# A two-layer graph network on one core: slot rows sent within SBUF in three parts of 14 slots, and attention one-hots, exponentials and sort halves on ScalarE and in PSUM

## The chip, the core and the metric

The kernel runs on one NeuronCore of a Trainium2 chip as a single program. The metric is the device time of an execution in microseconds. The times are compared as medians of repeated executions. A hardware profile of one execution gives the views that are quoted here. Engines are named as in the profile: PE is TensorE (PEld its weight loads), DVE is VectorE, ACT is ScalarE, POOL is GpSimd and SP is SyncE. POOL does no arithmetic in the loops below: it issues indirect DMAs (gathers of 128 rows by an index per partition).

## The reference

There are 12,500 nodes with 128 features and 200,000 edges, sorted by destination; all arithmetic is f32.

```python
h = relu(layernorm(x))
# layer 0: attention over the incoming edges, 8 heads of 16
q, k, v = h @ Wq.T, h @ Wk.T, h @ Wv.T
score = einsum('ehc,ehc->eh', q[dst], k[src]) / 4 + edge_attr @ We.T
alpha = softmax of score over the edges of one dst
x = x + segment_sum(v[src] * alpha, dst)
# layer 1: three graph convolutions on h = relu(layernorm(x)), 128 -> 256 -> 128 -> 128
#   conv(h) = D^-1/2 (A + I) D^-1/2 (h @ W) + b, then batch norm (and relu after the first two)
return x + that
```

## The kernel before

**Setup.** The nodes are cut into 106 tiles of 118 destinations (`TN`). Layer norm and the three projections run first and leave `q_d` and the joint table `kv_d` in HBM. Each tile has a window of 2048 edges (`WE`, 16 per partition, `JJ`), read at a position that is loaded into a register (L929).

**Attention** is one loop over the 106 tiles, in groups of four. Per tile:

- SP loads the edge features `ebx`, the tile-relative destinations `dw_b` (broadcast over the partitions) and `qt`. POOL issues 16 gathers of 1 KB rows into `kv` (L148). Three buffers of `kv` exist (pool `ga`).
- DVE writes the transposed one-hot `oht` from `dw_b` (L1013, 128x2048). PE spreads the queries to the edges with it (`qe`, L1019, 16 matmuls). DVE multiplies by the keys (L1020, four times 512 elements) and sums per head (L1023).
- PE adds the edge bias (L1036), and a chain of scans on DVE, small matmuls on PE and a copy on ACT finds each destination's maximum (L1051 to L1075).
- ACT writes the exponentials into `vals` (L1081). DVE multiplies the values by them (L1082, 2048 elements), which is the last reader of `kv`.
- DVE writes the one-hot `oh` (L677, called from `one_hot`), and PE sums over the edges (`acc`, L1089, 16 matmuls).

The order on each engine is fixed when the program is built, and each engine runs its own list strictly in order; instructions of neighbouring tiles are interleaved there.

Beside the last 80 tiles or so, **`place_edges`** sorts every tile's edges by source. It is a generator; `go_on(1)` at four places of a tile runs one step each. Its sort is a bitonic network on 106 partitions x 2048 keys, 66 stages, done twice. One stage is one step: a `min` and a `max` of 1024 elements each, both inputs in SBUF (L701, L702). Between the sorts, edges beyond `SB` = 13 per (tile, group of 128 sources) are marked late. Each tile has 98 x 13 = 1274 slots and up to `OV` = 768 late edges.

**Each convolution** (`conv_slots`, three times) works on blocks of nine tiles (`TB`), twelve blocks, with the table `hs` in SBUF:

- `take` (L1221 to L1228): for each of the 98 groups of 128 sources, DVE writes a one-hot `go` (128 x 117), PE multiplies (`gp`), so that row (tile, slot) holds the source's row. ACT copies four groups at a time into `stage`, and each 14 groups are written to a block `m` in HBM.
- `reduce`, for each tile of the block before: three DMAs read the tile's 1274 rows back from `m` into `mr` (L1245, 128 partitions x 10 rows), POOL gathers 6 x 128 late rows from the table in HBM (five buffers), DVE writes one one-hot `oh` of 16 x 118 (L1249), and PE adds 10 slot matmuls (L1253), 6 late ones (L1255) and the tile's own rows (L1159) into `zp`. After three tiles `finish` scales, applies the weights and takes statistics.
- `take` of a block and `reduce` of the block before are emitted interleaved; SP issues all their DMAs from one in-order list.

A f32 matmul stands as two instructions in the profile; "a pair" below is one matmul of the program.

## Time and profile before

| | us |
|---|---|
| median of 14 runs (lowest, highest) | 7413.61 (7369.84, 7436.9) |
| the profiled execution | 7384.13 |
| its span, first to last instruction | 7382.3 |
| attention, about | 190 to 3150 |
| three convolutions, about | 3200 to 7325 |

| busy over the span | us | share |
|---|---|---|
| PE | 4734.2 | 64% |
| DVE | 3410.5 | 46% |
| POOL | 4025.9 | 55% |
| ACT | 1014.7 | 14% |

The mean granted TensorE clock is 0.751 of full speed. The DMA engines move 1051.07 MB, 142 GB/s over the span; HBM sees 773.19 MB read and 272.26 MB written. The largest transfers are `m<-stage` (252 of 784 KB) and `mr<-m` (318 of 560 KB).

A line of the groups reads: line, engine, operation, output<-inputs, count | busy us, mean ns of one | idle time of the engine before it, with what ended it. A line of the windows gives, for a stretch of the span, its length and then the busy time of PE, PEld, DVE, ACT and POOL with the number of instructions in brackets, the granted PE clock, the DMA engines' share and GB/s. A line of the timeline gives start, duration, engine, line, operation and count.

### The profile page before, as it was taken

The numbers are of one execution on the slowest core, as the hardware profiler recorded it, in microseconds if no ns is written. First come the engines' busy times: TensorE is split into PE (matmuls) and PEld (weight loads), VectorE is DVE, ScalarE is ACT, GpSimd is POOL, SyncE is SP. The second block draws the span as 40 slices with busy tenths as digits, with TensorE's granted clock in tenths as the row PEclk, the third lists the DMA queues.
The fourth block names the chain that finished last, engine by engine and source line by source line (L and its number), as shares of the span: only waits on it lengthen the run. The fifth ranks groups of instructions, "written<-read, shape, count | busy, mean of one in ns | idle before, by whom it ended". The sixth has DMA issues, their size and how long they took to land. (4 is left out here: it accounts for less than half of the span.)

```text
span 7382.3 us, 80384 instructions
## 1 busy us (share of the span) xinstructions
PE 4734.2 (64%) x28564; PEld 4380.5 (59%) x28564; DVE 3410.5 (46%) x5972; ACT 1014.7 (14%) x2374; POOL 4025.9 (55%) x3617
## 2 busy tenths in 40 slices
PE   5665666566666666646666666666666666666666
PEld 2555565555556565646666666566666656666666
DVE  6455688878667755523332324223223233223234
ACT  2111111111011111111111110111111111111110
POOL 1566588888777877634444443344444425444443
PEclk8676766666776776678888888777777777778778
DMA  6444444444444445366666665565666656666666
GB/s 177 114 125 117 113 110 112 101 115 109 115 115 114 111 121 129 92 166 170 166 164 165 163 160 162 161 161 153 158 156 162 162 148 163 159 160 159 158 157 173
DMA packets 607714, 1051.07 MB, mean 142 GB/s; under 512 B 191227, under 2 KB 418491, under 8 KB 607201
## 3 DMA queue, kind: packets, MB, share of 16 engines
q1 hardware_dynamic: 464311, 695.85, 34.3%
q0 software_dynamic: 142608, 348.39, 19.5%
q8 instruction: 232, 3.80, 0.2%
q14 instruction: 175, 1.43, 0.1%
q10 hardware_dynamic: 388, 1.60, 0.1%
HBM read 773.19 MB, written 272.26 MB: 142 GB/s over the span
## 5 line engine op out<-in xcount | busy, mean ns | idle before, releaser
L148 POOL DMA_INDIRECT rows<-t_d,srcO x1908 | 1820.9, 954 | 2363.7 <-PE zp L1159 674.5
L148 POOL DMA_INDIRECT kv<-kv_d,srcA x1696 | 2200.7, 1298 | 777.7 <-issue 492.7
L1224 PE MATMUL gp<-hs,go 128*117 128x128 f32 x7056 | 1066.4, 309 | 756.3 <-issue 574.2
L1224 PEld LDWEIGHTS gp<-hs,go 128*117 128x117 f32 x7056 | 965.1, 209 | 842.3 <-issue 684.3
L1253 PE MATMUL zp<-oh,mr 128*128 128x118 f32 x6360 | 1062.2, 339 | 610.5 <-DMA mr<-m 324.4
L1253 PEld LDWEIGHTS zp<-oh,mr 128*128 128x128 f32 x6360 | 1021.2, 252 | 631.8 <-issue 318.1
L1249 DVE TENSOR_TENSOR oh<-nums,dlS 128x1888 f32<-128x1888 f32 x318 | 674.1, 2121 | 1479.8 <-PE zp L1255 1406.8
L1019 PE MATMUL qe<-qt,oht 128*128 128x128 f32 x3392 | 842.0, 412 | 227.0 <-issue 110.2
L1019 PEld LDWEIGHTS qe<-qt,oht 128*128 128x128 f32 x3392 | 769.4, 310 | 269.0 <-issue 165.0
L1221 DVE TENSOR_SCALAR go<-gi,iota_q 128x468 f32<-128x468 uint8 x1008 | 433.9, 456 | 1000.6 <-remote 459.5
L1226 ACT COPY stage<-gp 117x512 f32<-117x512 f32 x1008 | 522.5, 532 | 2290.6 <-PE gp L1224 775.3
L1089 PE MATMUL acc<-vals,oh 128*118 128x137 f32 x3392 | 556.2, 335 | 207.3 <-DVE vals L1082 167.9
L1089 PEld LDWEIGHTS acc<-vals,oh 128*118 128x118 f32 x3392 | 536.1, 230 | 230.7 <-DVE vals L1082 186.0
L1255 PE MATMUL zp<-oh,rows 128*128 128x118 f32 x3816 | 522.4, 287 | 45.7 <-issue 45.5
L1255 PEld LDWEIGHTS zp<-oh,rows 128*128 128x128 f32 x3816 | 496.2, 205 | 53.5 <-issue 52.8
L1020 DVE TENSOR_TENSOR kv<-qe,kv 128x512 f32<-128x512 f32 x424 | 288.1, 684 | 498.7 <-DMA kv<-kv_d,srcA 284.6
L1082 DVE TENSOR_TENSOR vals<-kv,vals 128x2048 f32<-128x2048 f32 x106 | 242.4, 2287 | 104.9 <-ACT vals L1081 61.8
L677 DVE TENSOR_TENSOR oh<-iota_f,dlA 128x1888 f32<-128x1888 f32 x106 | 224.0, 2114 | 126.2 <-remote 77.4
L1058 PE MATMUL ends<-ident,mg 128*8 128x128 f32 x212 | 52.0, 336 | 313.8 <-DVE mg L1053 244.8
L1023 DVE TENSOR_REDUCE sc<-kv 128x128 f32<-128x2048 f32 x106 | 240.8, 2272 | 0.0
L1036 PE MATMUL sm<-wbd,et 128*128 128x32 f32 x848 | 167.6, 351 | 94.1 <-DVE mg L1075 63.2
L1036 PEld LDWEIGHTS sm<-wbd,et 128*128 128x128 f32 x848 | 162.9, 283 | 101.0 <-issue 35.3
(242 smaller groups left out, 3544.1 us busy)
## 6 DMA issues: line engine op xcount, KB each, us to landing
m<-stage SPq DMA_DIRECT2D x252, 784.0 KB
mr<-m SPq DMA_DIRECT2D x318, 560.0 KB
dw_b<-dlb_d SPq DMA_DIRECT2D x106, 512.0 KB
gi<-gi_d SPq DMA_DIRECT2D x252, 204.8 KB
rows<-t_d,srcO POOLq DMA_INDIRECT x1908
kv<-kv_d,srcA POOLq DMA_INDIRECT x1696
ebx<-in_edge_attr_dram SPq DMA_DIRECT2D x106, 256.0 KB
mr<-m SPq DMA_DIRECT2D x318, 75.0 KB
```

The source lines that it names most:

```text
L148: nc.gpsimd.indirect_dma_start(out=o, out_offset=None, in_=table[:, :], in_offset=bass.IndirectOffsetOnAxis(ap=idx, axis=0))
L1019: nc.tensor.matmul(qe[:, k, :], ohv[:, :, j + k], qt, start=True, stop=True)
L1020: nc.vector.tensor_tensor(qk[:, j:j + 4, :], qe, qk[:, j:j + 4, :], op=ALU.mult)
L1036: nc.tensor.matmul(bias[:, 4 * k:4 * k + 4, :].rearrange("p j h -> p (j h)"), et[:, k, :], wbd, start=True, stop=True)
L1082: nc.vector.tensor_tensor(vh[:, :, :, :C], kv[:, :, D:].rearrange("p j (h c) -> p j h c", h=H), vh[:, :, :, C:].to_broadcast([P, JJ, H, C] ...
L1089: nc.tensor.matmul(acc, oh[:, j, :], va[:, j, :], start=(j == 0), stop=(j == JJ - 1))
L1221: nc.vector.tensor_scalar(go[:, :n], gv[:, a:a + n], iota_q, None, op0=ALU.is_equal)
L1224: nc.tensor.matmul(gp[:, i, :], go[:, i].rearrange("p t k -> p (t k)"), hs[:, g * SG + a + i, :], start=True, stop=True)
L1226: nc.scalar.copy(stage[:, a:a + n, :], gp[:, :n, :])
L1249: nc.vector.tensor_tensor(oh, nums.unsqueeze(1).to_broadcast(sh), dlS[:, t, :].unsqueeze(2).to_broadcast(sh), op=ALU.is_equal)
L1253: nc.tensor.matmul(zp[:, i, :], mr[:q, j, :], oh[:q, j, :], start=False, stop=False)
L1255: nc.tensor.matmul(zp[:, i, :], rows[:, j, :], oh[:, RC + j, :], start=False, stop=(j == JO - 1))
```

## The change

There are two halves.

**Attention.** `oht` and `oh` are made by ACT: absolute difference, then relu of one minus it (16 instructions of 118 elements for `oh`, whose bias differs per column). The exponentials go to PSUM (`ex`, in the tile of the bias), are multiplied from there, and are copied to `vals` by ACT afterwards. A sort stage copies the upper operand in two halves to PSUM (`hc`, ACT, 512 elements), and `min` and `max` run on 512 elements with that operand; each half is a step, and `go_on(2)` replaces `go_on(1)`. `acc` has one PSUM buffer instead of two, the bias tile two instead of one.

**Convolutions.** `SB` is 14, `OV` is 704 (the sixth gather has 64 rows); a tile has 98 x 14 = 1372 slots, a block still nine tiles. The 98 groups are cut into three parts of 45, 45 and 8 groups, in pieces of 5, 5 and 1 groups. The rows of a piece go by one SBUF-to-SBUF DMA from `stage` (126 partitions, slot and tile) to `mr` (14 partitions, every ninth or eighth one; the tile lies in the free dimension). There is no block in HBM any more. A part's rows of all nine tiles are one buffer of `mr`, of which there are two. `take` of a part is interleaved with `add` of the part before; `zp` of the block's three groups of tiles stays open in PSUM over the three parts. Gathers, own rows and `finish` come with the third part. The gathers' pool `ga` has three buffers instead of five.

```diff
-SB = 13
-OV = 768
+SB = 14
+OV = 704
+PARTS = ((0, 5, 9), (45, 5, 9), (90, 1, 8))
...
             def swap(lo, hi, lo2, hi2):
-                nc.vector.tensor_tensor(lo2, lo, hi, op=ALU.min)
-                nc.vector.tensor_tensor(hi2, lo, hi, op=ALU.max)
+                n, d = lo.shape[1:]
+                for k in range(2):
+                    cut = ...
+                    hc = ps.tile([P, WE // 4], FP, name="hc")[:NTT].rearrange(
+                        "t (n d) -> t n d", n=max(1, n // 2))
+                    nc.scalar.copy(hc, hi[cut])
+                    yield
+                    nc.vector.tensor_tensor(lo2[cut], lo[cut], hc, op=ALU.min)
+                    nc.vector.tensor_tensor(hi2[cut], lo[cut], hc, op=ALU.max)
...
+            def where_zero(x):
+                nc.scalar.activation(x, x, AF.Relu, bias=ones[:, 0:1], scale=-1.0)
...
-                    nc.vector.tensor_scalar(oht, dw_b, iota_q, None, op0=ALU.is_equal)
+                    nc.scalar.activation(oht, dw_b, AF.Abs, bias=niota[:, 0:1])
+                    where_zero(oht)
...
-                    go_on(1)
+                    go_on(2)
...
-                    nc.scalar.activation(vh[:, :, :, C], mx.rearrange("p h j -> p j h"), AF.Exp)
+                    nc.scalar.activation(ex, mx.rearrange("p h j -> p j h"), AF.Exp)
                     nc.vector.tensor_tensor(vh[:, :, :, :C], kv[:, :, D:].rearrange("p j (h c) -> p j h c", h=H),
-                                            vh[:, :, :, C:].to_broadcast([P, JJ, H, C]), op=ALU.mult)
+                                            ex.unsqueeze(3).to_broadcast([P, JJ, H, C]), op=ALU.mult)
+                    nc.scalar.copy(vh[:, :, :, C], ex)
...
-                    one_hot(oh, dlA[:, t, :])
-                    acc = ps2.tile([TN, H * (C + 1) + 1], FP, name="acc")
+                    for j in range(JJ):
+                        nc.scalar.activation(oh[:, j, :], iota_f[:, :TN], AF.Abs, bias=dlA[:, t, j:j + 1], scale=-1.0)
+                    where_zero(oh)
+                    acc = ps1.tile([TN, H * (C + 1) + 1], FP, name="acc")
...
+                def take(b, part, mr):
+                    _, n, pieces = PARTS[part]
+                    rows = mr[:pieces * SB, :, :n, :].rearrange("(k q) t c d -> q k t c d", k=SB)
+                    for _, q, m in batches[part]:
...
+                        stage = sg.tile([TS, MB, D], FP, name="stage")
+                        for a, c in groups(w, 4):
+                            go = gx.tile([P, 4, SB, TB], FP, name="go")
+                            nc.vector.tensor_scalar(go[:, :c], gv[:, a:a + c], iota_q, None, op0=ALU.is_equal)
+                            gp = pg.tile([TS, 4, D], FP, name="gp")
+                            for i in range(c):
+                                nc.tensor.matmul(gp[:, i, :], go[:, i].rearrange("p k t -> p (k t)"),
+                                                 hs[:, s0 + a + i, :], start=True, stop=True)
+                            nc.scalar.copy(stage[:, a:a + c, :], gp[:, :c, :])
+                        for i in range(m):
+                            nc.sync.dma_start(rows[q + i], stage[:, i * n:(i + 1) * n, :])
+                        yield
...
+                def add(b, part, mr):
...
+                        if part == 0:
+                            zps[t0] = pz.tile([P, GN, TN], FP, name="zp")
...
+                        if last:
+                            tg = own_rows(wk, table, t0, n)
+                        for t in range(t0, t0 + n):
...
+                            if last:
+                                rows = ga.tile([P, JO, D], FP, name="rows")
+                                for j, (_, r) in enumerate(over):
+                                    gather(rows[:r, j, :], table, srcO[:r, t, j:j + 1])
+                                nc.tensor.matmul(zp, tg[:, t - t0, :], ident[:TN, :TN], start=False, stop=False)
+                            for j in range(w):
+                                nc.tensor.matmul(zp, mr[:K, t % TB, j, :], oh[:K, j, :], start=False, stop=False)
+                            for j, (_, r) in enumerate(over if last else []):
+                                nc.tensor.matmul(zp, rows[:r, j, :], oh[:r, w + j, :], start=False,
+                                                 stop=(j == JO - 1 and t == t0 + n - 1))
+                            yield
+                        if last:
+                            finish(wk, t0, n, zps.pop(t0), use, ph)
...
+                for b in range(NBK):
+                    for part in range(len(PARTS)):
+                        mr = mt.tile([P, TB, MC, D], FP, name="mr")
+                        done = 0
+                        for g, _ in enumerate(take(b, part, mr)):
+                            while done < g * TB // (len(batches[part]) - 1):
+                                next(tiles, None)
+                                done += 1
+                        for _ in tiles:
+                            pass
+                        tiles = add(b, part, mr)
```

`place_edges` writes the slot indices in the new order (28 stores instead of 12), and the destinations of the slots in the order of the parts.

## The prediction

> **What bounds the kernel now.** I read the page first (shares, slices, groups), then windows of the two stages, the timeline inside each, the waits, and last the order of instructions of both kernels. The chain that ended last says nothing here: it is the output's last 0.5 us. No engine is busy over 64% of the span, so each stage is read by itself. The groups that carry it:
>
> ```profile
> L148 POOL DMA_INDIRECT rows<-t_d,srcO x1908 | 1820.9, 954 | 2363.7 <-PE zp L1159 674.5 <-PE gp L1224 519.7 <-issue 514.0
> L148 POOL DMA_INDIRECT kv<-kv_d,srcA x1696 | 2200.7, 1298 | 777.7 <-issue 492.7 <-DVE vals L1082 195.8 <-DVE rs L1122 51.2
> ```
>
> The reader is to see that one gather takes 954 ns in the convolutions and 1298 in the attention, though it issues the same 128 rows. The windows (attention before, during and after the sort; then one convolution):
>
> ```profile
> 200.00:800.00 600.00, 375.95 (x1858) 341.69 (x1858) 313.96 (x722) 73.63 (x262) 362.19 (x329) 0.70 0.46 117
> ...
> 1000.00:1800.00 800.00, 493.87 (x2488) 449.43 (x2488) 656.43 (x1003) 90.90 (x252) 666.25 (x440) 0.66 0.42 109
> ...
> 2600.00:3000.00 400.00, 268.21 (x1371) 241.60 (x1370) 226.41 (x426) 50.70 (x135) 294.86 (x247) 0.70 0.46 122
> ...
> 4900.00:5700.00 800.00, 519.22 (x3528) 500.08 (x3526) 233.87 (x303) 115.18 (x220) 364.73 (x383) 0.76 0.60 159
> ```
>
> POOL is the fifth of the pairs. Between two gathers stand 0.30 us in which POOL waits for nothing (the timeline's "[0.30 <-issue]"), so a gather occupies its duration plus 0.30. During the sort that is 666 + 440 x 0.30 = 798 of 800 us: **POOL is full**, at 28 tiles (L1082 runs 28 times there), 28.6 us a tile. After the sort it is 295 + 74 = 369 of 400, 26.7 us a tile. Before it, 362 + 99 = 461 of 600: there POOL waits for `kv` buffers, so the chain of PE, DVE and ACT sets the pace. Why gathers are slow shows in the timeline:
>
> ```profile
> 749.76 0.94 POOL L148 DMA_INDIRECT kv<-kv_d,srcA  x1 [0.30 <-issue]
> ...
> 750.51 1.28 DVE L1013 TENSOR_SCALAR oht<-dw_b,iota_q 128x2048 f32<-128x2048 bf16 x1
> ...
> 751.00 2.35 POOL L148 DMA_INDIRECT kv<-kv_d,srcA  x1 [0.30 <-issue]
> ...
> 753.66 0.95 POOL L148 DMA_INDIRECT kv<-kv_d,srcA  x1 [0.30 <-issue]
> ```
>
> The gather that falls on DVE's L1013 takes 2.35 us instead of 0.95. The same stands beside L677, L1082 and the sort's L701 and L702, which also read SBUF twice or at double rate; beside L1249, one of whose inputs lies in PSUM, gathers stay at 0.94.
>
> In the convolutions nothing is full (PE 65%, POOL 365 + 115 = 480 of 800, DMA 0.60). A block of 98 groups has 196 instructions of L1224, and 1384 of them lie in these 800 us: 7.06 blocks, **113 us a block**, 36 blocks. It is a loop of waits: the block goes to HBM and back, PE waits for `mr<-m` (up to 8.7 us at once in the waits), cools, and runs at half rate after it:
>
> ```profile
> 5206.08 4.59 PE L1253 MATMUL zp<-oh,mr 128*128 128x118 f32 x20 [6.16 <-issue]
> ...
> 5212.44 2.40 PE L1253 MATMUL zp<-oh,mr 128*128 128x118 f32 x20
> ```
>
> The same ten pairs cost 0.46 us each cold and 0.24 warm.
>
> **Attention: the parts.** *Removed from DVE, per tile:* L1013 1.28 and L677 2.11 us. L1082 stays at 2048 elements (2.29). A sort stage was 1.21 + 1.21 us, four a tile, 9.7; it becomes four instructions of 512, for which L1020 (512 elements, one input in PSUM, 684 ns) is the nearest row: 4 x 4 x 0.68 = 10.9. During the sort DVE has 656/28 = 23.4 us a tile now, so 23.4 - 3.4 - 9.7 + 10.9 = 21.2 then.
>
> *Added to ACT, per tile:* the rows are L1365 (354 elements with a bias per partition, 591 ns) and L1226 (512 elements 585, 256 elements 374, so 0.82 ns an element). That makes 591 + 1694 x 0.82 = 1.98 us for 2048 elements, twice; 0.40 for 118, sixteen times; 1.85 for 1888; 0.43 for the copy (L1081): 12.6 us. ACT has 90.9/28 = 3.2 now, so 15.8, and during the sort 8 copies of 0.585 more: 20.5.
>
> *POOL:* 16 x (0.945 + 0.30) = 19.9 us a tile if nothing slows it; PE has 494/28 = 17.6 at the clock granted now. Over all 1696 gathers the slowing costs 2201 - 1696 x 0.945 = 598 us: the most that attention can gain while POOL sets the pace.
>
> During the sort four engines then stand at 18 to 21 us and hand work to each other in order; `hc` has one buffer, so copy and min/max alternate. The tile can't be under 21.2; at 28.6 nothing is gained. I take 25, the middle: 34 tiles x 3.6 = **-122 us**. The sort still takes 33 tiles (twice the steps, twice the rate). After it, 48 tiles: slowed gathers cost 295 - 247 x 0.945 = 62 us on 15 tiles, 4.1 each; the waits for `kv` (31 us of 400) stay, and `place_edges`'s remaining steps, which keep both operands in SBUF, still slow some. I take 2.5: **-120**. Before the sort, 24 tiles: the chain sets the pace, DVE loses 3.4 us, ACT gains 12.6 and stands in it (`oht`, `th`, the exponentials, `att`, all in order): I take 0, between -3.4 and +4 (one ACT instruction of 2 us ahead of each of two links of the chain). Sum **-240**. Bounds: -598, and +240 if every copy of the sort waits 1 us behind a one-hot (21.2 + 8 = 29.2, no gain on 34 tiles) and the other 72 tiles get 3 us longer.
>
> **Convolutions: the parts.** *Removed:* per block 14 stores to HBM and 27 reads. *Added:* 26 SBUF-to-SBUF transfers, 126 x 98 x 512 B = 6.3 MB instead of 2 x 5.9. The row nearest to their rate is the hardware queue's total, 695.85 MB for 34.3% of 16 engines' span, 17.2 GB/s an engine; 6.3 MB is then 23 us of a block: hidden. *PE:* 98 + 9 x 18 = 260 pairs a block instead of 251. *DVE:* three one-hots a tile, 17 x 118 elements instead of 16 x 118, 30% busy: hidden. SP issues 49 DMAs a block instead of 57, but its list is in order, and in it the second part's pieces stand behind own-row loads that wait for PE.
>
> [...]
>
> *What is late next:* all 54 late gathers of a block now serve its third part, with three buffers. Three tiles are fetched ahead; the other six come one by one: 5 x 1.245 + 1.10 (64 rows; between 0.77 for half and 1.245) = 7.3 us, so 44, and about 5 for the last one's landing and its 8 pairs: **49 us** from the first tile's rows to the ninth's. By the order of instructions 108 pairs lie inside this stretch, 152 outside it. A pair costs 519/1764 = 0.294 us at the clock mix of now, so 32 (hidden) and 45. The second part's rows can only be sent when the third part of the block before has been read (three parts, two buffers), and PE then waits for the last copy and transfer: 6 us, between 0 and the 8.7 of today's wait, plus a little for two `stage` buffers. 49 + 45 + 6 = **100 us a block** instead of 113. I count 33 blocks, since each convolution's first and last run differently: 33 x 13.3 = **-440**. Bounds: all pairs warm and no wait, 49 + 37 + 2 = 88, -825; all 152 cold and 9 us of wait, 49 + 70 + 9 = 128, +485.
>
> **Sum.** 7384 - 240 - 440 = 6704, said as **6700 us**, against the profiled execution, which is 30 us under the median of the runs shown; that is inside the range.
>
> **Rivals.** *A: only the convolutions gain* (20%). ACT takes DVE's place in the chain. For it: in 200 to 800 POOL isn't the bound at all. Against: during the sort POOL is full and relieved for certain. 7384 - 440 + 0 = 6950. *B: both stages reach their floor* (17%). Cooling ends because PE's gaps shrink, and attention runs at 22 us a tile: 7384 - 500 - 750 = 6130. For it: today's block shows PE warm whenever it has a queue. *C: slower* (11%). One mechanism: the overflow stretch and the other two parts run one after the other, with POOL idle in the second and PE in gaps in the first, so PE stays cold. At 70 us for the 152 pairs plus waits the block is 128; from 120 us a block on, it eats attention's gain. 33 x 15 - 240 = +255 or, with no gain in attention, 7870. *D: gathers aren't relieved* (with A): the scans L1051 and L1078 also read SBUF twice. Against: gathers beside L1051 in the timeline stay at 0.95.
>
> **Chances.** Forecast 50%, A 20%, B 17%, C 11%, no change 2%. A measurement of this kernel can tell about 0.2% from none. Faster 0.87, same 0.02, slower 0.11. The range 6050 to 7400 leaves out C and the bottom of B.
>
> **What would show it.** Mean of the `kv` gathers at 0.95 to 1.05 us instead of 1298 ns: right on the slowing; at 1.2: wrong. L1082's successor running 32 times in 800 us of the sort: 25 us a tile. ACT busy over 55% in attention. 196 instructions of `gp` every 100 us; POOL's waits for `zp` gone from two parts and its gathers back to back in the third; HBM traffic down by some 420 MB. Wrong would be: `rows` waiting on `mr` transfers (SP's order), or DVE waiting for ACT's `hc` most of the sort.

## The result and the profile after

The changed kernel takes 8651.82 us (median of 10 runs, 8622.58 to 8669.75), the kernel before 7407.18 us (47 runs, 7364.33 to 7441.61): a ratio of 1.1674, 95% interval [1.1652, 1.1697]. The forecast was 6700 us and the range 6050 to 7400, so it failed in sign and in range. The profiled execution took 8649.76 us, its span 8648.0, the mean clock was 0.705. Attention ends at 3756 us instead of 3143 (+613), and the rest of the span has 4892 us instead of 4239 (+653): both halves lose.

From the page of the changed kernel, the two groups of gathers and the traffic:

```profile
HBM read 559.41 MB, written 60.93 MB: 72 GB/s over the span
...
L153 POOL DMA_INDIRECT rows<-t_d,srcO x1908 | 1811.5, 949 | 3048.4 <-PE zp L1312 2305.6
L153 POOL DMA_INDIRECT kv<-kv_d,srcA x1696 | 1686.4, 994 | 1889.0 <-DVE vals L1117 1081.7
```

The `kv` gathers fell from 1298 to 994 ns and HBM moves 425 MB less, as foretold; what the change was priced by did happen. But POOL, which was full in the sort, now waits 1889 us ahead of these gathers (778 before), and 3048 ahead of the others. The windows of the changed kernel (before, during and after the sort; then the convolutions; columns as above):

```profile
250.00:800.00 550.00, 278.11 (x1395) 249.53 (x1395) 188.74 (x515) 210.16 (x495) 242.86 (x256) 0.66 0.38 95
1200.00:2000.00 800.00, 410.42 (x2060) 369.66 (x2060) 455.34 (x922) 399.33 (x834) 360.53 (x370) 0.64 0.35 91
2800.00:3600.00 800.00, 437.80 (x2254) 395.09 (x2254) 278.31 (x649) 331.36 (x719) 379.58 (x400) 0.68 0.36 99
5700.00:6500.00 800.00, 515.72 (x3145) 472.28 (x3145) 255.34 (x391) 98.74 (x210) 313.96 (x331) 0.72 0.33 93
```

During the sort no engine is busy over 57%, ACT has 50%. A tile takes 34 us there (28.6 before), a block of a convolution 131.5 (113 before). Something waits for nothing that the page names. The timeline shows it; inside one unbroken run of 32 gathers (3014.7 to 3054.5):

```profile
3033.52 0.95 POOL L153 DMA_INDIRECT kv<-kv_d,srcA  x1 [0.30 <-issue]
3033.93 0.39 PE L1127 MATMUL acc<-vals,oh 128*118 128x137 f32 x1 [1.04 <-issue]
...
3036.07 0.39 PE L1127 MATMUL acc<-vals,oh 128*118 128x137 f32 x1 [1.75 <-issue]
...
3038.89 0.39 PE L1127 MATMUL acc<-vals,oh 128*118 128x137 f32 x1 [2.42 <-issue]
...
3040.30 0.69 DVE L1055 TENSOR_TENSOR kv<-qe,kv 128x512 f32<-128x512 f32 x1 [19.85 <-remote]
...
3058.50 0.29 DVE L1073 TENSOR_TENSOR sc<-sc,sm 128x128 f32<-128x128 f32 x1 [15.19 <-PE acc L1127]
...
3059.91 1.71 PE L1127 MATMUL acc<-vals,oh 128*118 128x137 f32 x6 [0.34 <-issue]
```

The 16 matmuls of `acc` (32 instructions) have nothing to wait for ("issue"). They should follow each other in 0.3 us, as the last six instructions do at 3059.91, once the run of gathers is over. The first 14 still do, from 3029.30 to 3032.9; the next ones in the list come every 2.1 to 2.8 us, and DVE stands still for 20 us for results of PE.

### The profile page after: what moved, and what is told of

The parts are those of the page before. It is cut to its first block, busy times and chain, and to the rows that moved or that the text cites. A ratio compares the mean times of both kernels' runs of the same rounds, so it can differ in the third digit from the quotient of the medians.

```text
span 8648.0 us, 85786 instructions
## 1 busy us (share of the span) xinstructions
PE 5140.9 (59%) x29309; PEld 4613.5 (53%) x29309; DVE 3428.6 (40%) x6812; ACT 2251.6 (26%) x4902; POOL 3502.2 (40%) x3617
## 4 chain that ended last, share of the span: by engine, by line
PE 23%; another core or an unknown queue 15%; issue 9%; DMA 3%; DVE 2%; ACT 2%; POOL 0%; SPq 0%; ACTq 0%; DVEq 0%; POOLq 0%
PE zp L1310 9%; PE gp L1273 6%; PE zp L1312 5%; ACT stage L1275 2%; DMA mr<-stage 1%; PE zp L1308 1%; DVE oh L1302 1%; DMA gi<-gi_d 1%; PE hq L1391 1%; PE tp L1372 1%; DVE go L1270 1%; POOL rows L153 0%; SPq L1277 0%; PE zp L1293 0%
## 5 line engine op out<-in xcount | busy, mean ns | idle before, releaser
L153 POOL DMA_INDIRECT kv<-kv_d,srcA x1696 | 1686.4, 994 | 1889.0 <-DVE vals L1117 1081.7
L1273 PE MATMUL gp<-hs,go 128*126 128x128 f32 x7056 | 1180.8, 326 | 916.7 <-ACT stage L1275 433.5
L1273 PEld LDWEIGHTS gp<-hs,go 128*126 128x126 f32 x7056 | 1048.0, 230 | 1128.2 <-ACT stage L1275 547.4
L1310 PE MATMUL zp<-oh,mr 126*128 126x118 f32 x6996 | 1152.1, 323 | 527.4 <-DVE oh L1302 263.7
L1310 PEld LDWEIGHTS zp<-oh,mr 126*128 126x128 f32 x6996 | 1067.3, 235 | 594.9 <-DVE oh L1302 305.9
L1275 ACT COPY stage<-gp 126x512 f32<-126x512 f32 (+2 forms) x1152 | 536.6, 487 | 3232.2 <-PE gp L1273 1289.7
L1302 DVE TENSOR_TENSOR oh<-nums,dlS 128x590 f32<-128x590 f32 (+1 forms) x954 | 813.2, 853 | 1317.0 <-remote 512.3
L1270 DVE TENSOR_SCALAR go<-gi,iota_q 128x504 f32<-128x504 uint8 (+2 forms) x1152 | 632.3, 569 | 1159.1 <-remote 592.6
L1312 PE MATMUL zp<-oh,rows 128*128 128x118 f32 x3816 | 674.7, 327 | 10.5 <-DMA rows<-t_d,srcO 8.5
L1123 ACT ACTIVATE oh<-iota_f,dlA 128x118 f32<-128x118 f32 x1696 | 513.0, 381 | 6.4 <-issue 6.4
L1117 DVE TENSOR_TENSOR vals<-kv,sm 128x2048 f32<-128x2048 f32 x106 | 241.6, 2279 | 14.7 <-ACT sm L1116 6.5
```

Source lines behind the costliest of these rows:

```text
L153: nc.gpsimd.indirect_dma_start(out=o, out_offset=None, in_=table[:, :], in_offset=bass.IndirectOffsetOnAxis(ap=idx, axis=0))
L1123: nc.scalar.activation(oh[:, j, :], iota_f[:, :TN], AF.Abs, bias=dlA[:, t, j:j + 1], scale=-1.0)
L1270: nc.vector.tensor_scalar(go[:, :c], gv[:, a:a + c], iota_q, None, op0=ALU.is_equal)
L1273: nc.tensor.matmul(gp[:, i, :], go[:, i].rearrange("p k t -> p (k t)"), hs[:, s0 + a + i, :], start=True, stop=True)
L1275: nc.scalar.copy(stage[:, a:a + c, :], gp[:, :c, :])
L1302: nc.vector.tensor_tensor(oh[:, :sh[1]], nums.unsqueeze(1).to_broadcast(sh), dl.unsqueeze(2).to_broadcast(sh), op=ALU.is_equal)
```

## What was asked

I measured this in every trace: **late** is the time from the end of the last recorded matmul that signals a semaphore to a semaphore update of PE that follows more than 0.12 us after it, added up without counting a moment twice. (Ends of matmuls are modelled and some records are missing, so it is rough. Counted from the last matmul of any kind, the 1108 and 2368 us below are 904 and 2049.) The kernels were measured on six occasions; on each of the five after the record, all ran on one chip, and the record doesn't name its chip. They fall into **two conditions**, and without this the numbers can't be read:

| | with hold-ups | without |
|---|---|---|
| occasions | the record; runs 9 to 12; runs 13 to 16 | runs 1 to 4; 5 to 8; 17 and 18 |
| the kernel before | 7407; 7291; 7308 | 6164; 6153; 6149 |
| late, kernel before | 1108 us | 8 or less |
| late, changed kernel | 2368 us | 8 or less |

One chip was in both (runs 1 to 4 and 13 to 16). The spans differ by 7382.3 - 6147.1 = 1235 us for the kernel before and 8648.0 - 6216.8 = 2431 for the changed one, so late is about as long as most of it (1108 and 2368). By stage it is rougher:

| us | attention with / without | cost, late | rest with / without | cost, late |
|---|---|---|---|---|
| before | 3143 / 2950 | 193, 385 | 4239 / 3197 | 1042, 718 |
| changed | 3756 / 2587 | 1169, 1093 | 4892 / 3630 | 1262, 1275 |

Part of a cost can be the clock, which is lower with hold-ups: 0.76 in the prediction's window of a convolution, 0.89 in run 6's. Slower work is not the difference: in the kernel before, a `kv` gather takes 1298 ns with and 1329 without, and L1082 on DVE 2287 and 2286.

The theories:

- **Hold-up.** While POOL issues gathers without a pause, PE's completions come late. Gathers stretched by DVE broke the runs up and so protected the kernel before; the change took that away in attention, and in the convolutions put a block's gathers into one part.
- **The chain through ACT** (my bounds, Rival A): ACT's one-hots and copies simply make a tile longer.
- **The serial stretch** (Rival C): the ninth tile's gathers come after the others, and POOL then idles through two parts.

## The experiments

The runs stand in the order in which they were made. "With" and "without" name the condition.

### 1. A probe of runs of gathers (probe_runs, without)

The probe is a program by itself; it computes nothing of the reference. Its round is four matmuls into PSUM and a DVE copy of 512 elements, 24 times, beside 24 gathers on POOL; stages alter the gathers, here with rests between them.

```diff
+for j in range(24):
+    gather(kv[:, j, :], wide)   # then, by stage: nothing, or an iota
+for _ in range(24):
+    for i in range(4): nc.tensor.matmul(q[:, i, :], ident, rhs, start=True, stop=True)
+    nc.vector.tensor_copy(cp, q)
```

> A measurement by itself: it leaves the whole graph network out. TensorE and VectorE hand one PSUM buffer to each other (four matmul pairs, one copy of 512 elements, 24 rounds a stage) while POOL gathers 128 rows 24 times, in several manners. Theory 1 (a long unbroken run of gathers holds up TensorE's completions): alone a round is about 2 us; beside 24 gathers of 1 KB rows back to back the first five to eight rounds are as when alone, and from about 10 us after the first gather until about 3 us after the last one rounds take 4 us and more; a rest of about 0.4 us behind each gather lessens this, rests of about 1 us, or of 2 us behind each fourth gather, or DVE instructions that slow the gathers, take it away. Theory 2 (the lateness comes from the kernel's own order, the gathers only happen to run then): rounds are within 20% of the lone ones in every stage.

1393.85 us. A round took 2.9 us in every stage, alone or beside gathers: nothing came late. The rests had been moved ahead of the gathers by the order of the program, so they rested nothing. By itself this spoke against the hold-up; it was the first sign of the second condition.

### 2. The attention half alone (attn_half, without)

The kernel before with all hunks of the diff outside `conv_slots` and its constants.

```diff
-nc.vector.tensor_scalar(oht, dw_b, iota_q, None, op0=ALU.is_equal)
+nc.scalar.activation(oht, dw_b, AF.Abs, bias=niota[:, 0:1])
+where_zero(oht)
...
-go_on(1)
+go_on(2)
```

> The attention half of the change alone, convolutions as before. The trace of the whole change has its attention 598 us longer than before (end of the last gather of kv at 3720 instead of 3122 us). If the halves don't act on each other, both theories give 7384 + 600 = 7980 us, with 34 us a tile and kv gathers at 0.95 us. By theory 1 the time in which TensorE's completions are late in attention rises from about 310 to about 950 us; theory 2 says nothing on this.

5801.94 us, 0.9409 [0.9388, 0.9429] of before on the same chip: 362 us faster. The 7980 us that I expected from the record's losses did not come.

### 3. The convolution half alone (conv_half, without)

The changed kernel with the old attention.

```diff
-nc.scalar.activation(oht, dw_b, AF.Abs, bias=niota[:, 0:1])
+nc.vector.tensor_scalar(oht, dw_b, iota_q, None, op0=ALU.is_equal)
```

> The convolution half of the change alone, attention as before. In the trace of the whole change a block takes 131.5 us instead of 113, and the three convolutions 656 us more: 7384 + 656 = 8040 us if the halves don't act on each other. By theory 1 the late time of TensorE's completions is about 130 us in each 500 us of the convolutions instead of 75.

6614.35 us, 1.0726 [1.0705, 1.0748]: 451 us slower, with 8 us late in all. So this half loses by a cause of its own.

### 4. Rests behind each gather (after_rests, without)

```diff
 gather(kv[:, j, :], kv_d, srcA[:, t, j:j + 1])
+rest(pause)          # an iota on POOL
```

> The changed kernel, with work for POOL that nothing needs behind each gather: one iota of 384 elements (about 0.44 us) in attention, four of 16 elements (about 0.13 us each) in the convolutions. POOL so has 16 x 0.45 = 7 us more to do in each tile of attention and 54 x 0.5 = 27 us more in each block. Theory 1: broken runs hold TensorE up less; attention goes from 34 towards 30 us a tile (-400 us), a block from 131.5 to about 122 (-300), 7950 us in all. Theory 2: nothing is won in attention, and the stretch of gathers, which is a block's longest, grows by up to 27 us: 8650 to 9600 us.

8249.76 us, 1.3373 [1.3351, 1.3396]. The test was spoiled: the iotas were gathered into long bunches (from 3500 to 3700 us POOL does nothing else), the first two blocks took 417 and 238 us, the later ones 95.6 as without rests. The 0.44 and 0.13 us expected for an iota follow POOL's iotas in the trace before (0.13 us for 1 element, 0.23 for 128, 1.83 for 2048); here the 9328 iotas took 0.21 us on average. Nothing follows from it.

### 5. The changed kernel again (after_again, without)

No edit.

> The changed kernel once more, beside the kernel before on the same chip. The halves were timed on a chip where the kernel before took 6164 us instead of 7407 and where TensorE's completions were never late. If the lateness belongs to the chip, the changed kernel gives there 6164 - 362 (attention half) + 450 (convolution half) = 6250 us, 1.01 times the kernel before, with conv blocks of about 95 us and attention 360 us shorter; on a chip with the lateness it gives about 1.17 again, as in the first measurement.

6224.26 us, 1.0118 [1.0097, 1.0139]. The halves add up: 6153 - 362 + 451 = 6242. So the same kernel is 1.2% slower in one condition and 16.7% in the other.

### 6. The kernel before, profiled here (before_here, without)

No edit.

> The kernel before, to have its trace from the same chip. Where TensorE's completions are late inside long runs of gathers: 7400 us, blocks of 113 us. Where they are not: about 6160 us, blocks of 82 to 85 us as in the attention half alone, attention as in the convolution half alone.

6148.88 us. Six blocks of a convolution, first of this kernel, then of after_again:

```profile
4215.00:4705.00 490.00, 388.07 (x3012) 379.29 (x3011) 195.09 (x258) 95.76 (x186) 310.13 (x325) 0.89 0.85 219
```

```profile
4097.00:4664.00 567.00, 469.30 (x3143) 426.18 (x3142) 255.53 (x391) 99.03 (x210) 309.61 (x324) 0.83 0.46 131
```

The block before is 490/6 = 82 us, not 113; the changed one is 567/6 = 95. Where they go, in the waits of after_again in this stretch and in its timeline:

```profile
POOL rows L153 <- PE zp L1312: 162.9, 15, 27.8
```

```profile
4104.61 0.96 POOL L153 DMA_INDIRECT rows<-t_d,srcO  x1 [27.41 <-PE zp L1312]
```

A block has a third part of some 52 us (4102 to 4154, from the late matmuls of its first tile to those of its ninth), as long as POOL needs to fetch tiles four to nine, and then some 43 us of the two other parts. In these POOL fetches the next three tiles (its 54 gathers are one run of 68 us, 4104.6 to 4172.5) and then waits 27.4 us at once, for the buffers that only the next third part reads: the serial stretch, with the clock at 0.83 instead of 0.89.

### 7. The late edges spread over the parts (spread, without)

Each part takes the gathers and late pairs of every third tile, so POOL has work in all three.

```diff
+now = t % len(PARTS) == part
...
-if last:
+if now:
     rows = ga.tile([P, JO, D], FP, name="rows")
     for j, (_, r) in enumerate(over):
         gather(rows[:r, j, :], table, srcO[:r, t, j:j + 1])
...
-for j, (_, r) in enumerate(over if last else []):
+for j, (_, r) in enumerate(over if now else []):
```

(The late one-hots have a tile of their own; `ohs` has 3 buffers, `gy` 3 instead of 4.)

> The changed kernel with the late edges' gathers and matmuls spread over the three parts (tile t with part t mod 3) instead of all in the third; the one-hots of slots and of late edges are made apart. Theory 3 (a block of the changed kernel is the stretch in which POOL gathers for all nine tiles, about 47 us, and then the rest, about 48 us, one after the other): with a third of the gathers in each part they lie beside the other parts' matmuls and a block falls from 95 to between 78 and 86 us, 400 us less in all. Theory 4 (the loss is SP's order and the transfers from stage to mr): a block stays at 92 to 98 us.

5706.57 us, 0.9281 [0.926, 0.9302]; late 8 us. The serial stretch is shown: without it a block takes 79 us (six in 472), and POOL's waits for `zp` fall from 162.9 to 63.2 us:

```profile
3936.00:4408.00 472.00, 412.20 (x3138) 385.56 (x3137) 261.08 (x444) 100.36 (x210) 314.03 (x324) 0.93 0.57 157
```

```profile
POOL rows L153 <- PE zp L1313: 63.2, 12, 7.1
```

In this condition it beats both kernels.

### 8. The probe with gathers released by a copy (probe_again, without)

The probe, with stages in which a gather's index is first copied into one of 1, 2, 4 or 8 buffers, which limits the gathers in flight.

```diff
+ix = pool.tile([P, 1], I32, name="ix")
+nc.scalar.copy(ix, idx)
+nc.gpsimd.indirect_dma_start(out=kv[:, j, :], in_=wide, in_offset=...(ap=ix, axis=0))
```

> A measurement by itself; it leaves the whole graph network out. As the probe before (24 rounds between TensorE and VectorE beside 24 gathers), but with gathers held apart by the number of index buffers: one, two, four or eight gathers in flight. On a chip without the lateness every round takes 2.9 us, as in the first probe. On one with it, rounds beside back-to-back gathers grow to 4 us and more from about 10 us after the first gather, and with one or two gathers in flight they stay at 2.9.

1411.48 us; every round 2.9 us. Again nothing came late in this condition.

### 9 and 10. Attention's half, less one of its parts (attn_no_onehot, attn_no_halves, with)

From attn_half, the one-hots go back to DVE; or the sort goes back to whole stages in SBUF.

```diff
 # attn_no_onehot
-nc.scalar.activation(oht, dw_b, AF.Abs, bias=niota[:, 0:1])
-where_zero(oht)
+nc.vector.tensor_scalar(oht, dw_b, iota_q, None, op0=ALU.is_equal)
 # attn_no_halves
-nc.scalar.copy(hc, hi[cut])
-nc.vector.tensor_tensor(lo2[cut], lo[cut], hc, op=ALU.min)
+nc.vector.tensor_tensor(lo2, lo, hi, op=ALU.min)
```

> The attention half alone, with both one-hots made by VectorE again (exponentials and sort halves in PSUM stay). On the chips without lateness the attention half took 362 us off the kernel before (0.941). Theory 3a (the gain is gathers that VectorE no longer slows, and 3.4 us less of VectorE): two of the slowing instructions come back, 1.28 and 2.11 us a tile, kv gathers have a mean of about 1150 ns, and half of the gain goes: 0.965 to 0.975 of before. Theory 3b (the gain is the sort alone): 0.94 as with them. On a chip with the lateness theory 1 has the one-hots on VectorE break the runs: faster than the attention half there.

> The attention half alone, with the sort as before (1024 elements, both inputs in SBUF, one step a place). Theory 3a: tiles 28 to 56, which run beside the sort, go from 22.3 us back to 26 to 28 us, the other tiles keep 21 to 22: the sort's part of the gain, 28 x 5 = 140 us and something of the second sort, goes: 0.965 to 0.975 of before. If the sort's part is nothing: 0.94.

7662.88 us, 1.0513 [1.0457, 1.057], and 7605.56 us, 1.0407 [1.0351, 1.0464], against 7290.53. The groups of attn_no_onehot, then of attn_no_halves:

```profile
L148 POOL DMA_INDIRECT kv<-kv_d,srcA x1696 | 1869.8, 1102 | 1433.1 <-DVE vals L1096 832.2
```

```profile
L148 POOL DMA_INDIRECT kv<-kv_d,srcA x1696 | 1766.1, 1041 | 1459.8 <-DVE vals L1091 764.6
```

| | mean of a `kv` gather | late in attention | attention ends |
|---|---|---|---|
| before (the record) | 1298 ns | 385 us | 3143 us |
| attn_no_onehot | 1102 | 696 | 3480 |
| attn_no_halves | 1041 | 919 | 3413 |
| changed (the record) | 994 | 1093 | 3756 |

The half loses without either of these parts: the first run has no one-hot on ACT, the second no copies of sort halves. The shorter the gathers, the more comes late. Both runs keep some of the chain through ACT, so they don't rule it out; run 2 speaks against it, where the whole of it made attention shorter (2600 us, 2950 in run 6) and nothing was late. ACT's instructions in attention grow in the order of the rows too (1212, 1579, 3335, 3596), so the rows alone don't part the gathers from the number of instructions. The second row speaks for the gathers: all instructions together grew by 2% there, and late from 385 to 696 us.

### 11. The spread kernel again (spread_again, with)

No edit.

> The changed kernel with the late edges spread over the three parts, once more. On a chip without lateness 0.928 of before again. On one with it (before near 7400) theory 1 predicts shorter runs of gathers than in the changed kernel in the convolutions, so 1.167 falls to between 1.05 and 1.12, attention being as in the changed kernel.

7969.84 us, 1.0915 [1.0861, 1.0969]: better than the changed kernel, worse than before. Late is 2034 us, a block takes about 113.

### 12. The probe again (probe_third, with)

The stages of 8, and more of them.

> The probe with one, two, four or eight gathers in flight once more; it leaves the whole graph network out. On a chip without lateness every round takes 2.9 us. On one with it rounds beside back-to-back gathers grow to 4 us and more, those beside one or two gathers in flight don't.

1601.92 us. Now rounds come late. The timeline of the plain run of gathers:

```profile
93.54 1.10 POOL L59 DMA_INDIRECT kv<-in_x_dram,idx  x1 [92.18 <-DVE idx L56]
...
104.12 2.08 PE L69 MATMUL q<-rhs,ident 128*128 128x128 f32 x8 [0.78 <-DVE cp L70]
...
106.24 0.69 DVE L70 COPY cp<-q 128x512 f32<-128x512 f32 x1 [2.17 <-PE q L69]
...
111.84 0.69 DVE L70 COPY cp<-q 128x512 f32<-128x512 f32 x1 [4.92 <-remote]
...
112.59 2.08 PE L69 MATMUL q<-rhs,ident 128*128 128x128 f32 x8 [3.53 <-issue]
...
122.37 0.69 DVE L70 COPY cp<-q 128x512 f32<-128x512 f32 x1 [9.84 <-remote]
```

The first 12 us of the run cost nothing (rounds of 2.9 us). Then PE's instructions stand at their place in 2.08 us, but the DVE copy behind them starts 4.9 and 9.8 us after the end of its predecessor. In the first of two passes rounds reach 10.5 us beside the 1 KB gathers, 12.6 beside 512 B ones, 14.7 beside 64 rows; 14.0 and 16.1 with four and eight in flight; and 2.9 us, undisturbed, with two in flight (a gather every 1.6 us), with one, and beside 24 plain transfers of SP. Rounds of ACT and DVE alone, with few instructions, stay at 1.2 to 1.3.

### 13. The changed kernel a third time (after_third, with)

No edit.

> The changed kernel beside the next three on their chip: 1.17 of before (near 7300 to 7400) on a chip with the lateness, 1.01 of before (near 6150) on one without.

8507.51 us, 1.1643 [1.1554, 1.1733]; late 2229 us. The record repeats, on the chip of runs 1 to 4.

### 14. Two gathers in flight in attention (attn_two, with)

From attn_half:

```diff
+ixs = ctx.enter_context(tc.tile_pool(name="ixs", bufs=2))
...
+ix = ixs.tile([P, 1], I32, name="ix")[:o.shape[0]]
+nc.gpsimd.tensor_copy(ix, idx)
-gather(kv[:, j, :], kv_d, srcA[:, t, j:j + 1])
+gather(kv[:, j, :], kv_d, ix)
```

> The attention half alone, with at most two gathers in flight in attention: each gather takes its indices from one of two small buffers, filled by a POOL copy just before, so it waits for the last but one to land. By the probe a gather then comes every 1.6 us instead of 1.25, 16 of them take 26 us. On a chip with the lateness, theory 1: no late completions in attention, 26 to 28 us a tile instead of 34, 7290 to 7400 - 100 to 250 us, so 0.965 to 0.99 of before, though POOL has more to do and every gather is later than in the attention half. If the lateness isn't what costs the time: 34 us a tile or more and 1.07 or more. On a chip without it: POOL sets the pace at 26 to 27 us a tile instead of 22, 0.99 to 1.02 of before.

7770.06 us, 1.0628 [1.0571, 1.0686]. Of the 660 us that are late none lies in attention any more, yet it ends at 3582. The timeline of POOL tells why:

```profile
1200.34 0.18 POOL L155 COPY ix<-srcA 128x1 int32<-128x1 int32 x1 [0.90 <-DMA kv<-kv_d,ix]
1200.79 0.97 POOL L148 DMA_INDIRECT kv<-kv_d,ix  x1 [0.27 <-POOL ix L155]
...
1206.52 0.18 POOL L155 COPY ix<-srcA 128x1 int32<-128x1 int32 x1 [1.17 <-DMA kv<-kv_d,ix]
```

Waiting for a landing, the copy and the gather make one every 2.07 us instead of the 1.6 that I took from the probe: 16 x 2.07 = 33 us a tile. The expectation (0.965 to 0.99) failed. On the same chip the changed kernel's attention ends at 3682 (run 13) and, without hold-ups, at 2587: nearly all that pacing removes is paid for pacing.

### 15. Two in flight everywhere (spread_two, with)

The same edit on spread, for both kinds of gathers.

> The spread version with at most two gathers in flight in attention and in the convolutions. A block's 54 gathers then take about 87 us. On a chip with the lateness, theory 1: blocks of 90 to 95 us instead of about 120, attention 26 to 28 us a tile, 6600 to 6900 us or 0.90 to 0.95 of before, faster than both kernels. If the lateness isn't the cause: not under 1.09, what the spread version took there. On a chip without it: blocks of 88 to 92 instead of 79 to 84, 6300 to 6500 us, 1.02 to 1.06 of before.

7754.96 us, 1.0617 [1.0558, 1.0676]. Late fell from 2034 (run 11, on another occasion) to 29 us, and the time only by 215; 0.90 to 0.95 had been expected. The line of POOL's copies in the groups, with their waits for landings:

```profile
L160 POOL COPY ix<-srcO 128x1 int32<-128x1 int32 x1908 | 399.3, 209 | 1046.5 <-DMA rows<-t_d,ix 961.9 <-issue 17.2 <-PE gp L1280 14.3
```

A block is 54 x 2.07 = 112 us, a tile 33: POOL sets the pace. That two in flight stop the late completions is shown; what they cost the kernel by themselves is not.

### 16. Which work is held up (probe_kinds, with)

Stages of the probe with other work beside the run of gathers, and with shorter runs.

```diff
+for i in range(8): nc.vector.tensor_copy(ca[...], cp[...])   # "small": DVE and ACT, no TensorE
+nc.tensor.matmul(q, identb, rhsb, ...)                       # "bf16": one matmul a round
+run(n)                                                       # n of 6, 8, 10, 12, 16
```

> A measurement by itself; it leaves the whole graph network out. Beside 24 gathers back to back: rounds of four float32 pairs with VectorE (as before, 2.9 us, late from the fifth round on where there is lateness); of one pair; with ScalarE as the reader; of one bfloat16 matmul of 512 columns; a stream of 120 pairs with no reader; eight small VectorE copies and one of ScalarE a round, without TensorE; a DMA and a VectorE copy a round; then four pairs beside only 6, 8, 10, 12 and 16 gathers. If matmul completions as such are held, all rounds with TensorE are late, one pair and bfloat16 too, and the others not. If it is the number of instructions, the rounds of one bfloat16 matmul stay as they are and the eight small copies become late. By the first trace the lateness needs about eight gathers: none beside 6, some beside 10 and more.

1350.11 us. Four pairs a round: up to 12.6 us. One pair a round: from 1.2 to 4.2. ACT as the reader: up to 11.9. A stream of pairs: 16 instructions in 1.8, then 20.2 us. One bf16 matmul a round: 1.4, never late. Eight small DVE copies a round, no TensorE at all: from 1.5 to 9.1 us. That fits a hold-up of engines that complete many instructions and not of PE as such, though the stages differ in more than the count. Beside 6, 8 and 10 gathers nothing came late, beside 12 one round (4.2), beside 16 some (up to 7.0). In the first pass the four pairs were not late at all in their first stage; but its gathers were not one run: five of them came 6.1 us apart, each after a landing, and at most 11 followed each other at 1.25 us.

### 17 and 18. Three and eight in flight (spread_three, spread_eight, without)

```diff
-ixs = ctx.enter_context(tc.tile_pool(name="ixs", bufs=2))
+ixs = ctx.enter_context(tc.tile_pool(name="ixs", bufs=3))   # and 8
```

> The spread version with three index buffers, so at most three gathers in flight, each behind a POOL copy of its indices: 0.97 + 0.27 + 0.19 + 0.1 = 1.54 us a gather at least, 24.6 us for a tile's 16, 83 us for a block's 54. On a session with the lateness (before near 7300), theory 1: few late completions (under 400 us in all), 26 to 29 us a tile, blocks of 90 to 100, 6700 to 7100 us, 0.92 to 0.97 of before. If what it gains is nothing beside two in flight: 1.06 again. On a session without the lateness (before near 6150): 25 to 26 us a tile, blocks of 84 to 88, 6000 to 6200 us, 0.97 to 1.01.

> The same with eight index buffers, so that the copies remain and nothing waits for a landing: 1.54 us a gather in a run. With the lateness, theory 1: gathers at 1.54 instead of 1.25 us hold the others up less than in the spread version (1.09) but more than with three in flight, 0.95 to 1.05 of before, 400 to 1500 us of late completions. Without it, as with three in flight or a little faster.

6810.04 us, 1.1077 [1.1058, 1.1095], and 6341.95 us, 1.031 [1.0293, 1.0327]. The chip was in the condition without hold-ups, so they show only the price of pacing: against 5707 for spread, 635 us with eight buffers, where the copies still wait 485 us for landings, which I had ruled out, and 468 more with three. For this condition I had expected 0.97 to 1.01 of before; both missed it.

## Why the prediction was wrong

**The step that failed.** "7384 - 240 - 440 = 6704" took the durations of one trace for properties of the work, and it has no term for what gathers do to other engines. A tile of the sort took 34 us, where I had 25 and, if nothing was gained, 28.6; a block took 131.5 us, where I had 100 and 128 at most. By comparison with the other condition, 1235 us of the trace before were a hold-up. It grew when gathers followed each other more densely (late in attention 385 us at a mean of 1298 ns a gather, 1093 at 994), and the change makes them denser. I set POOL at 19.9 us a tile and never asked what else that would do.

The sign stood in the trace before. "PE waits for `mr<-m`" was read beside a line that says `[6.16 <-issue]`, a wait with no named cause. PE's longest waits in 4900 to 5700, 7.06 blocks:

```profile
PE gp L1224 <- issue: 113.9, 38, 6.2
PE zp L1253 <- issue: 65.9, 13, 6.2
PE zp L1253 <- DMA mr<-m: 59.6, 8, 8.7
```

The same kernel in run 6 (4215 to 4705, six blocks):

```profile
PE zp L1253 <- DMA mr<-m: 79.7, 14, 7.5
PE zp L1253 <- issue: 20.1, 4, 5.1
```

The waits for `mr<-m` are in both, 8 and 13 us a block. Those without a named cause were 25 us a block and fell to 3. Like for like and in the record's condition, the +1266 us are:

| | without hold-ups | cost of hold-ups, changed less before | sum |
|---|---|---|---|
| attention | 2587 - 2950 = -363 | 1169 - 193 = +976 | +613 |
| the rest | 3630 - 3197 = +433 | 1262 - 1042 = +220 | +653 |

**Attention, -240.** The mechanism was right where there is no hold-up: -363, and 0.9409 for the half alone. It shows in one row: beside L1082, which reads SBUF twice, a gather of the kernel before has a median of 2.02 us; beside the same multiply with one input in PSUM (L1117 of the changed kernel) it has 0.95. The sizes were low: by the starts of the value multiplies a tile fell from 28.6 to 22.4 us in the sort (I took 25) and from 24.2 to 21.7 before it, where I took 0 for fear of ACT in the chain; after it from 25.5 to 23.0, the 2.5 that I took. ACT was 75% busy in the sort (602 of 800 us) and not the bound.

In the record the share of time late grows with the gathers started in the last 10 us: in the sort of the kernel before 0 up to five, 0.04 for six and 0.24 for eight; in the sort of the changed kernel 0.01 or less up to four, 0.19 for five, 0.50 for six, 0.63 for eight. Stretched gathers came less often: in attention the time with eight in the last 10 us rose from 388 to 1126 us. The count isn't the whole rule. At six the two kernels differ more than tenfold, and run 15, in which gathers wait for landings, spends 2.2 ms at six with next to nothing late. "POOL's slowing costs 598 us: the most that attention can gain" was beside the point: by this reading it also bought something.

**Convolutions, 113 to 100 us a block.** The new block was foretold well for a chip without hold-ups: 49 + 45 + 6 = 100 against a measured 52 + 43 = 95. The old one was the mis-sized term. "It is a loop of waits" explained 113 us by the way through HBM; 82 to 85 of them are the block, the other 30 are the condition. So the half loses some 12 us a block (433 / 36) where I had it gain 13. In the record a block takes 131.5 us: the third part grows to 76 us (5751 to 5827), in three runs of 18 gathers, and after two of them POOL waits 9 to 11 us for late matmuls. In the changed kernel's convolutions 0.50 of the time is late after five gathers in 10 us, 0.65 after six. Its waits in six blocks (5746 to 6538):

```profile
POOL rows L153 <- PE zp L1312: 392.5, 24, 45.3
ACT stage L1275 <- remote: 210.9, 30, 15.4
```

The longest wait of POOL is the serial stretch, longer now (45 us at once). ACT's 211 us for `remote` I read as PE's lateness; in six blocks without hold-ups (4097 to 4664 of run 5) ACT has no such wait.

**Transfers, 23 us hidden.** Right: 19% of 16 engines' time for the 2560 B packets (20.2 to 20.5 GB/s) and about 2% for the third part's 512 B ones (4% with the own rows, which are no part of this) over 95 us is 20 us a block, beside other work. That 16 engines share them was an assumption of the 23 us; no run here shows how many did, and nothing hung on it.

**Rivals.** C had the right side and a right mechanism: the parts do run one after the other, and run 7 removes that. But it was priced on cold matmuls (0.46 us a pair, 128 us a block; the granted clock of before was 0.50 in 5206.0 to 5210.7, where the pairs took 0.46, and 1.00 in 5212.4 to 5214.9, where they took 0.24), and it gives only the +433 of the convolutions. The hold-up was not among them; its cost makes the other +1196 (976 + 220), against -363 that attention gains. D fell: the gathers were relieved, and by the reading above that did the harm. A and B fell with the forecast.

**What would show it.** `kv` gathers at 994 ns and HBM traffic down 425 MB: seen. POOL's gathers back to back in the third part: three runs of 18, and one of 54 without hold-ups. 32 tiles in 800 us of the sort: 23, and 35 without hold-ups. ACT over 55%: 50%, and 75%. A block every 100 us: 131.5, and 95.

**What stays open.** That runs of gathers and late completions go together, by dose and by probe, and that two in flight remove them, is shown. That they make the whole +1196 rests on the two conditions and on sums that agree to 10% and 3% (by the stricter count to 27% and 16%); the runs that removed them also slowed POOL, so no run gives their price alone. The change also gives ACT more instructions to complete, and no run varied that alone. What sets the condition is unknown; it isn't the chip. All executions were taken with the profiler, and nothing here tells whether that matters.

## What to carry to other kernels

Before a stall is priced, ask whether the same trace shows results that come late for no named reason: gaps of "issue" inside a list of ready matmuls, readers released by "remote" long after the producer's end. Here such time belonged to the condition of the run and to what other engines did, and an edit that made indirect gathers follow each other faster enlarged it (late 1108 us before, 2368 after it, 8 or less in the other condition). And take the baseline again beside each experiment: here the same pair of kernels gave 1.012 and 1.167; the best version, late gathers spread over the parts, gave 0.928 without hold-ups and 1.092 with them, and no version that was run with them beat the kernel before (the attention half alone was not).

## What the runs showed of the hardware

- In one condition, from some 12 us into the probe's unbroken run of 128-row gathers (one every 1.25 us, run 12), other engines' instructions and completions came late: DVE's copies 4.9 and 9.8 us after the end of the one before, rounds of up to 10.5 us instead of 2.9. In the changed kernel of the record DVE waited 20 us for PE's results, and matmuls came late until some 5 us after the run of gathers (3054.5 to 3059.9).
- In run 16 nothing was late beside 6, 8 and 10 gathers, and one round (4.2 us) beside 12. In run 12 rounds reached 12.6 us beside 512 B rows and 14.7 beside 64 rows, and stayed at 2.9 beside plain transfers.
- With two gathers in flight (one every 1.6 us in the probe, 2.07 in the kernel) it vanished: 29 us late instead of 2034.
- It isn't bound to TensorE: eight small DVE copies and one of ACT, without a matmul, went from 1.5 to 9.1 us a round, while one bf16 matmul a round stayed at 1.4 (run 16).
- Gathers were longer beside some DVE work. In the kernel before, the gathers that overlap L1082 and L677, whose two inputs lie in SBUF, have a median of 2.02 and 2.49 us, those that overlap the sort's L701 and L702 1.60 and 1.63, and those that overlap L1013 (2048 elements in 1.28 us, where L1082 takes 2.29) 1.79, with 2.35 in the line shown. With DVE idle a gather took 0.94 us, and beside L1117 of the changed kernel, L1082 with one input in PSUM, 0.95. Relieved of most of it, the mean fell from 1298 to 994 ns.
